# A selective-scan convolution block: another order of the small and full TensorE tiles, four PSUM banks in rotation, and three pieces of work moved between engines

## The chip, the cores and the metric

The kernel runs on one core of a Trainium2 chip. The metric is the device time of one execution in microseconds. A core has the engines TensorE (PE; its weight loads are shown apart as PEld), VectorE (DVE), ScalarE (ACT), GpSimd (POOL) and the DMA queues of SyncE (SP). Matmul results lie in PSUM, which this kernel uses as eight banks of 512 float32 for each of 128 partitions.

## The reference, cut to what matters

The input is `x` of shape (4, 128, 96, 96), float32. It is normalized by groups and flattened to sequences of 9216 positions in four directions (rows forward and back, columns forward and back). Each sequence goes through the block below; the four results are put back in place, multiplied by `fuse_w` and added to `x`.

```python
B, DIM, H, W = (4, 128, 96, 96)
HID, MH, G, K = (256, 32, 4, 5)
t = _grouped1x1(x, in_proj_w, in_proj_b, G)
u, gate = (t[:, :HID], t[:, HID:])
u = silu(u)
u = depthwise_conv(u, dw_w)                     # 5 taps along the sequence
s = _conv1x1(u, ssm_in_w)
a = DMIN + (DMAX - DMIN) * sigmoid(_conv1x1(u, ssm_delta_w, ssm_delta_b))
a = clip(a, 0.0001, 0.9999)
bb = tanh(_conv1x1(u, ssm_b_w, ssm_b_b))
cc = tanh(_conv1x1(u, ssm_c_w, ssm_c_b))
# hst[l] = a[l] * hst[l-1] + bb[l] * s[l]       (written with cumsum of logs)
u = u + _conv1x1(cc * hst + ssm_d[None, :, None] * s, ssm_out_w)
u = _grouped1x1(u * sigmoid(gate), mix_w, mix_b, G)
return _conv1x1(u, out_proj_w, out_proj_b)
```

## The kernel before

The weights of the last three products (mix, out_proj, fuse) are multiplied once at the start into `w_fin`. The work is then cut into units of N = 384 positions by 128 or 256 channels. Two units of opposite direction, s = 0 and s = 1, make a pair; there are 192 pairs, 48 per batch element, and `p` counts the four pairs of a step, on whose end a scan over the step's positions depends. In each batch element the first 24 pairs ("V") go along columns, the last 24 ("H") along rows. The loop is software pipelined: pair t does the convolution, projections and the scan's inputs of pair t, the output side (gate, `ssm_out`, gating) of pair t - LAG with LAG = 6, and the final product of the pair before that.

The order of each engine is that of the program text (it is scheduled by hand). A matmul of `mm` uses 32 columns of the array; its height is that of the operand: 32 rows in `rows` and `ssm_out`, 128 or 64 in `conv`, 128 in `proj` and `accumulate`. A float32 matmul shows as two records in the trace. All the `mm` calls are on one line, L129.

```python
SSM, TAPS, GATE = 0, 0, (2, 3)          # psum banks
REST = ((4, 5), (6, 7))

def rows(i, bi, banks):                 # in_proj: front half of unit i, gate of unit bi
    ...
    for c in range(4):
        for j in range(2):
            if i is not None:
                ...
                mm(bank(banks[0][j]), c, wn[r, 32 * m : 32 * m + 32], x_in[s][r, q, :], True, True)
            if bi is not None:
                ...
                mm(bank(banks[1][j]), c, gwn[r, 32 * c : 32 * c + 32],
                   x_in[bu["s"]][r, gq, off : off + N], True, True)
    # then on ScalarE: two Tanh of the gate into gv (L359), two Silu into sil (L370)
    ...

def ssm_out(bi):                        # 16 matmuls of 32x32 into banks 0 to 3
    ...

def add_u(bi):                          # L399, both units in one instruction
    pz = psum[:, SSM : SSM + 4, :N]
    nc.vector.tensor_add(pz, pz, us[bi].rearrange("p s j n -> p (s j) n"))

def gating(bi, s):                      # L404
    v = units[bi + s]["v"]
    pz = psum[:, SSM + 2 * s : SSM + 2 * s + 2, :N]
    nc.vector.scalar_tensor_tensor(v, v, 1.0, pz, ALU.add, ALU.mult)

def conv(i, banks):                     # half of the channels: band matmuls, then two copies to u (L426)
    ...

def taps(i, ks):                        # the other half: tap 0 on ScalarE (L440), taps 1 to 4 on DVE (L442),
    part = psum[:, TAPS : TAPS + 2, :N] # with the partial sum in banks 0 and 1
    ...

def proj(i, banks):                     # B, a, s and C of the pair
    ...                                 # 16 matmuls, then
    nc.scalar.activation(ta[:, p, :], pa, AF.Tanh, bias=b_proj[:, 0:1])              # L468, ta has a stride of R = 4
    nc.scalar.copy(tb[0:64, p, :], pb[0:64, :])                                      # L469, s
    nc.scalar.activation(tb[64:P, p, :], pb[64:P, :], AF.Tanh, bias=b_proj[64:P, 1:2])  # L470
    ...
    nc.gpsimd.tensor_scalar(a, a, half, DMIN + half, ALU.mult, ALU.add)              # L473
    nc.gpsimd.tensor_scalar(a, a, 0.9999, 0.0001, ALU.min, ALU.max)                  # L474
    nc.gpsimd.tensor_mul(ta[0:64, p, :], tb[0:64, p, :], ta[0:64, p, :])             # L475
    nc.gpsimd.tensor_scalar_mul(tb[0:64, p, :], tb[0:64, p, :], d_sb[0:64, :])       # L476, d*s

def scan(step, part):                   # DVE, L494: half a step, in the first two pairs of the next step
    ...
def outputs(step, p):                   # GpSimd, L500 to L502: C*h, + d*s, a copy
    ...

def accumulate(bu, bk):                 # the product with w_fin, added to acc in SBUF
    ...
    y, add = py[:, :N], nc.vector.tensor_add
    if s == 0:                          # unit s = 0: copy out (L517 or L519), add on GpSimd
        ys = wk.tile([P, N], F32, tag="ys", name=f"ys_{bu['id']}")
        ...
        y, add = ys, nc.gpsimd.tensor_add
    else:                               # unit s = 1 ("r"): add on DVE out of PSUM
        y, p, st = y[:, ::-1], R - 1 - p, NS - 1 - st
    ...                                 # L528 ("V") or L532 ("H")

def pair(t):
    i, k, bi = 2 * t, t % R, 2 * (t - LAG)
    ...
    front_banks, conv_banks = REST[t % 2], REST[1 - t % 2]
    rows(front, back, (front_banks, GATE))
    taps(i, range(1, K))
    conv(i, conv_banks)
    recurrence(t)                       # scan (k < 2) and outputs
    ...
    rows(front + 1, bi + 1, (front_banks, GATE))
    if waiting and (bi == 2 or (bi - 2) % (NU // B)):
        accumulate(waiting.pop(0), conv_banks[0])
        if len(waiting) > 1 and units[bi]["st"] == 1:
            accumulate(waiting.pop(0), conv_banks[1])
    ssm_out(bi)
    add_u(bi)
    if later:                           # a piece of the next batch element's statistics
        small[0] = front_banks[1]
        next(later[0], None)
    for s in range(2):
        gating(bi, s)
    proj(i, (conv_banks[1], front_banks[0]))
    first_tap(i + 2)
    if waiting:
        accumulate(waiting.pop(0), front_banks[1])
    waiting.extend(units[bi : bi + 2])
```

(In `pair` the tests for the first and last pairs are cut.) When a batch element is done, its result is written from `acc` to memory and `acc` is loaded with the next one's `x`; the `if` before the first `accumulate` puts off the first unit of a new batch element, and the one below it catches up a few pairs later.

Of the kernel before, what the change touches and what calls it, by code (L numbers as in the profile page):

```python
# [34 lines left out]
F32 = mybir.dt.float32  # L35
I32 = mybir.dt.int32
AF = mybir.ActivationFunctionType
ALU = mybir.AluOpType

P = 128  # L40
B, DIM, HH, WW = 4, 128, 96, 96
# [3 lines left out]
DMIN, DMAX = 0.999, 0.9999  # L45
# [5 lines left out]
N = LN * WW // R  # L51
M = WW // R
LAG = 6
# [4 lines left out]
def conv_preact_kernel(  # L58
# [20 lines left out]
    nc = tc.nc  # L79
# [16 lines left out]
    units = []  # L96
# [19 lines left out]

    psum = ps.tile([P, 8, 512], F32, name="psum")
    SSM, TAPS, GATE = 0, 0, (2, 3)  # L120
    REST = ((4, 5), (6, 7))
    LAST = ((4, 5), (6, 7))

    def bank(i):
        return psum[:, i, :]

    def mm(o, col, lhsT, rhs, start, stop):
        r = slice(32 * col, 32 * col + 32)
        nc.tensor.matmul(o[r, : rhs.shape[-1]], lhsT, rhs, start=start, stop=stop,  # L129
                         skip_group_check=True)  # L130
# [263 lines left out]
                    mm(bank(SSM + 2 * s + j), c, w_so[r, 128 * j + 32 * c : 128 * j + 32 * c + 32],  # L394
                       z[r, p, :], True, True)

    def add_u(bi):
        pz = psum[:, SSM : SSM + 4, :N]
        nc.vector.tensor_add(pz, pz, us[bi].rearrange("p s j n -> p (s j) n"))  # L399

    def gating(bi, s):
        v = units[bi + s]["v"]
        pz = psum[:, SSM + 2 * s : SSM + 2 * s + 2, :N]
        nc.vector.scalar_tensor_tensor(v, v, 1.0, pz, ALU.add, ALU.mult)  # L404

    us = {}

    def conv(i, banks):

        un = units[i]  # L410
        sil, p = sils[un["step"]], un["p"]
        small = 1 if p < 2 else 0

        def part(s, k, g, r, start):
            mm(bank(banks[s]), g, band[r, s, p, k, g, :], sil[r, s, 0, g, k : k + N],
               start, not start)

        for s in range(2):
            for g in range(4):
                part(s, 1 - small, g, slice(0, P), True)  # L420
        for g in range(4):
            for s in range(2):
                low = 64 * ((small + s + 1) % 2)
                part(s, small, g, slice(low, low + 64), False)
        for s in range(2):
            nc.scalar.copy(us[i][:, s, 0, :], bank(banks[s])[:, :N])  # L426
# [27 lines left out]
    def proj(i, banks):  # L454

        step, p = units[i]["step"], units[i]["p"]
        if step not in scans:
            scans[step] = [
                wk.tile([P, N, R], F32, tag="t0", name=f"t0_{step}").rearrange("p n r -> p r n"),
                wk.tile([P, R, N], F32, tag="t1", bufs=3, name=f"t1_{step}"),  # L460
            ]
        ta, tb = scans[step]
        for j in (1, 0):
            for bk, cols in zip(banks, ((qb, qb, qa, qa), (qs, qs, qc, qc))):
                for c in range(4):
                    mm(bank(bk), c, w_proj[:, j, cols[c]], us[i][:, c % 2, j, :], j == 1, j == 0)
        pa, pb = (bank(bk)[:, :N] for bk in banks)
        nc.scalar.activation(ta[:, p, :], pa, AF.Tanh, bias=b_proj[:, 0:1])  # L468
        nc.scalar.copy(tb[0:64, p, :], pb[0:64, :])  # L469
        nc.scalar.activation(tb[64:P, p, :], pb[64:P, :], AF.Tanh, bias=b_proj[64:P, 1:2])  # L470
        a = ta[64:P, p, :]
        half = (DMAX - DMIN) / 2
        nc.gpsimd.tensor_scalar(a, a, half, DMIN + half, ALU.mult, ALU.add)  # L473
        nc.gpsimd.tensor_scalar(a, a, 0.9999, 0.0001, ALU.min, ALU.max)  # L474
        nc.gpsimd.tensor_mul(ta[0:64, p, :], tb[0:64, p, :], ta[0:64, p, :])  # L475
        nc.gpsimd.tensor_scalar_mul(tb[0:64, p, :], tb[0:64, p, :], d_sb[0:64, :])  # L476

    def first_tap(i):
        if i < NU:
            new_u(i)  # L480
            taps(i, range(1))
# [21 lines left out]

    reload = []

    def accumulate(bu, bk):
        b, s, p, st = bu["b"], bu["s"], bu["p"], bu["st"]
        py = bank(bk)
        for j in range(2):
            for c in range(4):  # L510
                mm(py, c, w_fin[:, bu["dir"], j, 32 * c : 32 * c + 32], bu["v"][:, j, :],
                   j == 0, j == 1)
        y, add = py[:, :N], nc.vector.tensor_add
        if s == 0:
            ys = wk.tile([P, N], F32, tag="ys", name=f"ys_{bu['id']}")
            if bu["order"] == "V":
                nc.scalar.copy(ys, y)  # L517
            else:
                nc.scalar.activation(ys, y, AF.Identity, bias=b_fin)  # L519
            y, add = ys, nc.gpsimd.tensor_add  # L520
        else:
            y, p, st = y[:, ::-1], R - 1 - p, NS - 1 - st
        if bu["order"] == "V":
            part = acc.rearrange("p (m q) r c -> p m q r c", q=R)[
                :, :, p, :, bass.ds(st * LN // R, LN // R)
            ]
            y = y.rearrange("p (c r m) -> p m r c", r=R, m=M)
            add(part, y, part)  # L528
            return
        part = acc[:, bass.ts(st, LN), p, :]  # L530
        y = y.rearrange("p (h m) -> p h m", m=M)
        add(part, y, part)  # L532
        if bu["st"] >= NS // 2 and bu["p"] == R - 1:

            halves = [bass.ts(2 * st + e, LN * WW // 2) for e in range(2)]
            for r in halves:
                nc.sync.dma_start(out[b, :, r], accf[:, r])
            reload.extend(halves)
            if s == 1:
                if b + 1 < B:  # L540
                    for r in reload:
                        nc.sync.dma_start(accf[:, r], xr[b + 1, :, r])
                reload.clear()
# [6 lines left out]
    def recurrence(t):  # L550
        i, k = 2 * t, t % R
        if k < 2 and 0 <= t // R - 1 < NU // UB:
            scan(t // R - 1, k)
        if 0 <= i - 10 < NU:
            outputs(units[i - 10]["step"], units[i - 10]["p"])

    def pair(t):
        i, k, bi = 2 * t, t % R, 2 * (t - LAG)
        front = i + UB if i + UB < NU else None
        back = bi if bi >= 0 else None  # L560
        front_banks, conv_banks = REST[t % 2], REST[1 - t % 2]
        rows(front, back, (front_banks, GATE))
        taps(i, range(1, K))
        conv(i, conv_banks)
        recurrence(t)
        un = units[i]
        if un["order"] == "V" and un["b"] + 1 < B and k > 1:
            for e in range(2):
                stats_chunk(un["b"] + 1, un["st"] * R + 2 * (k - 2) + e)
            if un["st"] == NS - 1 and k == R - 1:  # L570
                later[:] = [stats_finish(un["b"] + 1, nc.gpsimd)]
        if back is None:
            first_tap(i + 2)
        if front is not None or back is not None:
            rows(None if front is None else front + 1, None if back is None else bi + 1,
                 (front_banks, GATE))

        if waiting and (bi == 2 or (bi - 2) % (NU // B)):
            accumulate(waiting.pop(0), conv_banks[0])
            if len(waiting) > 1 and units[bi]["st"] == 1:  # L580
                accumulate(waiting.pop(0), conv_banks[1])
        if back is not None:
            ssm_out(bi)
            add_u(bi)
            if later:
                small[0] = front_banks[1]
                next(later[0], None)
            for s in range(2):
                gating(bi, s)
        proj(i, (conv_banks[1], front_banks[0]))  # L590
        if back is not None:
            first_tap(i + 2)
        if waiting:
            accumulate(waiting.pop(0), front_banks[1])
        if back is not None:
            waiting.extend(units[bi : bi + 2])

    def last_pair(t):

        bi = 2 * (t - LAG)  # L600
        recurrence(t)
        for s in range(2):
            rows(None, bi + s, (None, LAST[s]))
        ssm_out(bi)
        add_u(bi)
        for s in range(2):
            if len(waiting) > 1 - s:
                accumulate(waiting.pop(0), LAST[0][s])
            gating(bi, s)
        waiting.extend(units[bi : bi + 2])  # L610

# [6 lines left out]
    with tc.manual_schedule(  # L618
        engines={nc.tensor.engine, nc.vector.engine, nc.scalar.engine, nc.gpsimd.engine}
    ):  # L620
        for t in range(NU // 2):
            pair(t)
        for t in range(NU // 2, NU // 2 + LAG):
            last_pair(t)
        for s in range(2):
            accumulate(waiting.pop(0), LAST[0][s])


_NAMES = [
# [75 lines left out]
```

## Time and profile before

| | |
|---|---|
| time, median of 3 runs | 2121.9 us (2120.81 to 2121.96) |
| span of the profiled execution | 2121.0 us |
| granted TensorE clock | 0.994 |
| PE busy | 2074.4 us, 37072 matmul records |
| DVE busy | 1814.4 us |
| POOL busy | 1732.4 us |
| ACT busy | 1557.4 us |
| DMA | 133.89 MB, mean 63 GB/s |

The profile is of one execution. Its page gives the busy time of each engine, the span in 40 slices, the DMA queues, the chain of work that ended last (followed back from the last instruction, at each step to what released it), and the costliest groups of instructions: line, engine, operation, tiles written and read, shape, count, then busy time in us, the mean of one in ns, and the idle time of the engine just before them with what ended it. Finer views are the timeline (instructions of one engine in order of time: start, length, engine, line, operation, tiles, count, and idle time before), the waits (who waited for whom, in us, times, longest), and the groups. Ends of matmuls are modelled, and a PE that is called busy may still be filling or draining. Starts are the safer numbers.

### The profile page before, as it was taken

What the parts mean: (1) busy time and instruction counts of PE and PEld (TensorE: products, weight loads), DVE (VectorE), ACT (ScalarE), POOL (GpSimd) and SP (SyncE); (2) the same over time, 40 slices, a digit from 0 to 9 for tenths busy, and PEclk for the clock granted to TensorE, in tenths of its full rate; (3) what the DMA queues carried; (4) which work ended last, traced back from release to release, by engine and by line L of the source; (5) the groups of instructions that cost most, each with busy time, mean ns of one, the idle gap of its engine ahead of it and who ended that gap; (6) DMA issues with size and microseconds to landing.
All of it is one profiled execution on the core that took longest, in us unless ns stands there. A gap on an engine that the chain in (4) does not pass through costs nothing.

```text
span 2121.0 us, 83902 instructions
## 1 busy us (share of the span) xinstructions
PE 2074.4 (98%) x37072; PEld 666.1 (31%) x37072; DVE 1814.4 (86%) x1786; ACT 1557.4 (73%) x2899; POOL 1732.4 (82%) x1717
## 2 busy tenths in 40 slices
PE   5999999999999999999999999999999999999998
PEld 3233333333333333333332333333333333333323
DVE  4699998888888998888898899888888788888886
ACT  3777777777777777777777777777777677777763
POOL 4688888888887888888878888888888788888885
PEclk7999999999999999999999999999999999999999
DMA  5121211111542221111343221111134211111111
GB/s 159 50 66 51 58 51 43 36 44 46 149 128 59 58 64 38 39 41 44 96 117 108 59 67 42 43 37 44 36 103 125 71 36 44 38 43 36 36 50 71
DMA packets 83403, 133.89 MB, mean 63 GB/s; under 512 B 11616, under 2 KB 70624, under 8 KB 83040
## 3 DMA queue, kind: packets, MB, share of 16 engines
q1 hardware_dynamic: 81024, 127.64, 22.4%
q8 instruction: 291, 4.77, 1.0%
q10 hardware_dynamic: 2016, 0.90, 0.2%
q14 instruction: 72, 0.59, 0.1%
HBM read 109.62 MB, written 18.87 MB: 61 GB/s over the span
## 4 chain that ended last, share of the span: by engine, by line
PE 92%; DVE 3%; ACT 2%; POOL 1%; DMA 1%; issue 0%; ACTq 0%; SPq 0%; POOLq 0%; DVEq 0%
PE psum L129 91%; DVE t L494 1%; DVE psum L399 1%; DVE gv L404 1%; ACT t L468 0%; ACT sil L370 0%; DMA acc<-in_xr 0%; POOL t L475 0%; DMA b_mix<-in_mix_b 0%; ACT psum L440 0%; DVE psum L442 0%; POOL t L476 0%; POOL t L500 0%; POOL t L473 0%; POOL t L474 0%
## 5 line engine op out<-in xcount | busy, mean ns | idle before, releaser
L442 DVE SCALAR_TENSOR_TENSOR psum<-sil,w_tap,psum 128x768 f32<-128x768 f32 x576 | 589.1, 1023 | 103.3 <-ACT psum L440 89.3
L129 PE MATMUL psum<-gv,w_fin 128*32 128x384 f32 x6144 | 568.7, 489 | 1.3 <-DVE mean L177 1.0
L129 PE MATMUL psum<-u,w_proj 128*32 128x384 f32 x6144 | 536.5, 489 | 4.9 <-ACT sil L370 2.7
L359 ACT ACTIVATE gv<-psum,bnorm 128x384 f32<-128x384 f32 x768 | 403.2, 577 | 91.8 <-PE psum L129 79.3
L468 ACT ACTIVATE t<-psum,b_proj 128x384 f32<-128x384 f32 x192 | 193.9, 1010 | 369.6 <-PE psum L129 356.6
L129 PE MATMUL psum<-sil,band 128*32 128x384 f32 (+1 forms) x6144 | 445.4, 495 | 0.2
L399 DVE TENSOR_TENSOR psum<-psum,u 128x1536 f32<-128x1536 f32 x192 | 339.2, 1767 | 122.3 <-PE psum L129 62.8
L129 PE MATMUL psum<-x_in,wn 32*32 32x384 f32 (+1 forms) x12288 | 432.0, 498 | 7.2 <-DVE gv L404 4.2
L370 ACT ACTIVATE sil<-psum,bnorm 128x385 f32<-128x385 f32 x768 | 404.9, 587 | 13.0 <-DMA xs<-in_xr 10.8
L500 POOL TENSOR_TENSOR t<-t,t 64x384 f32<-64x384 f32 x192 | 242.6, 1264 | 155.6 <-DVE t L494 146.3
L404 DVE SCALAR_TENSOR_TENSOR gv<-gv,psum 128x768 f32<-128x768 f32 x384 | 349.4, 950 | 6.4
L501 POOL TENSOR_TENSOR t<-t,t 64x384 f32<-64x384 f32 x192 | 290.6, 1514 | 15.0
L129 PEld LDWEIGHTS psum<-gv,w_fin 128*32 128x32 f32 x6144 | 180.3, 109 | 343.1 <-issue 220.5
L129 PEld LDWEIGHTS psum<-u,w_proj 128*32 128x32 f32 x6144 | 179.8, 109 | 343.5 <-issue 309.4
L473 POOL TENSOR_SCALAR t<-t 64x384 f32<-64x384 f32 x192 | 187.1, 975 | 100.2 <-ACT t L468 88.6
L476 POOL TENSOR_SCALAR t<-t,d_sb 64x384 f32<-64x384 f32 x192 | 240.5, 1253 | 19.8
L475 POOL TENSOR_TENSOR t<-t,t 64x384 f32<-64x384 f32 x192 | 237.0, 1234 | 15.4
L129 PEld LDWEIGHTS psum<-sil,band 128*32 128x32 f32 (+1 forms) x6144 | 114.5, 107 | 318.1 <-issue 276.3
L129 PEld LDWEIGHTS psum<-x_in,wn 32*32 32x32 f32 x12288 | 124.5, 103 | 286.0 <-ACT sil L370 117.6
L129 PE MATMUL psum<-t,w_so 32*32 32x384 f32 x6144 | 198.0, 493 | 4.2 <-POOL t L500 3.9
L442 DVE SCALAR_TENSOR_TENSOR u<-sil,w_tap,psum 128x768 f32<-128x768 f32 x192 | 194.9, 1015 | 6.8
L474 POOL TENSOR_SCALAR t<-t 64x384 f32<-64x384 f32 x192 | 184.2, 960 | 15.9
(73 smaller groups left out, 1455.3 us busy)
## 6 DMA issues: line engine op xcount, KB each, us to landing
x_in<-in_xs SPq DMA_DIRECT2D x96, 385.0 KB, 4.3
x_in<-in_xs SPq DMA_DIRECT2D x384, 96.2 KB, 2.5
acc<-in_xr SPq DMA_DIRECT2D x48, 384.0 KB, 4.2
out<-acc SPq DMA_DIRECT2D x48, 384.0 KB, 3.2
xs<-in_xr SPq DMA_DIRECT2D x72, 192.0 KB, 3.1
w_fuse<-in_fuse_wT ACTq DMA_DIRECT2D x1, 256.0 KB, 7.3
w_proj<-in_proj_wT ACTq DMA_DIRECT2D x1, 128.0 KB, 4.8
w_so<-in_ssm_out_wT ACTq DMA_DIRECT2D x1, 128.0 KB, 2.6
```

The costliest lines, as they stand in the source:

```text
L129: nc.tensor.matmul(o[r, : rhs.shape[-1]], lhsT, rhs, start=start, stop=stop, skip_group_check=True)
L359: nc.scalar.activation(gv[:, j, :], bank(banks[1][j])[:, :N], AF.Tanh, bias=gbn[:, 2 + j : 3 + j], scale=0.5,)
L370: nc.scalar.activation(sil[:, j, g, :], bank(banks[0][j])[:, : N + 1], AF.Silu, bias=bn[:, 1:2] if j else bn[:, 4 + g : 5 + g],)
L399: nc.vector.tensor_add(pz, pz, us[bi].rearrange("p s j n -> p (s j) n"))
L404: nc.vector.scalar_tensor_tensor(v, v, 1.0, pz, ALU.add, ALU.mult)
L442: nc.vector.scalar_tensor_tensor(us[i][:, :, 1, :] if k == K - 1 else part, src, w_tap[:, k : k + 1], part, ALU.mult, ALU.add,)
L468: nc.scalar.activation(ta[:, p, :], pa, AF.Tanh, bias=b_proj[:, 0:1])
L473: nc.gpsimd.tensor_scalar(a, a, half, DMIN + half, ALU.mult, ALU.add)
L475: nc.gpsimd.tensor_mul(ta[0:64, p, :], tb[0:64, p, :], ta[0:64, p, :])
L476: nc.gpsimd.tensor_scalar_mul(tb[0:64, p, :], tb[0:64, p, :], d_sb[0:64, :])
L500: nc.gpsimd.tensor_mul(ta[0:64, p, :], tb[64:P, p, :], ta[64:P, p, :])
L501: nc.gpsimd.tensor_add(tb[0:64, p, :], ta[0:64, p, :], tb[0:64, p, :])
```

## The change

The change orders the work of a pair anew and moves three pieces of it.

- The first `accumulate` of a pair goes ahead of the second `rows`, into bank 2 (`GATE[0]`), and `ssm_out` comes directly behind that second `rows`: two bursts of 32x32 tiles without full tiles in between.
- Banks 4 to 7 go round by one a pair instead of being swapped by twos. The gate of the second `rows` goes to the banks of `conv`, and `proj` uses these two as well.
- `add_u` is gone; `gating` adds u for its own unit, so that there are two additions of half the size, each in front of its product.
- The product d*s moves from GpSimd to ScalarE and into the next pair (`scale_s`), behind the second `rows`.
- In the loop the unit s = 1 ("r") is now also copied out by ScalarE and added on GpSimd, not on DVE. In the last pairs (`direct`) the addition is on DVE.
- The first Tanh of `proj` goes to a new contiguous tile `tm`; the three instructions behind it read `tm` and write `ta`.
- `proj` begins with j = 0 instead of j = 1, and `first_tap` of the next pair comes ahead of `proj`.
- At a batch change the late unit is caught up with at the end of the same pair (`late`), and the statistics' pieces run only in pairs without a scan, behind `proj`.

```diff
-    SSM, TAPS, GATE = 0, 0, (2, 3)
-    REST = ((4, 5), (6, 7))
+    SSM, TAPS, GATE, REST = 0, 0, (2, 3), 4
...
-    def add_u(bi):
-        pz = psum[:, SSM : SSM + 4, :N]
-        nc.vector.tensor_add(pz, pz, us[bi].rearrange("p s j n -> p (s j) n"))
-
     def gating(bi, s):
         v = units[bi + s]["v"]
         pz = psum[:, SSM + 2 * s : SSM + 2 * s + 2, :N]
+        nc.vector.tensor_add(pz, pz, us[bi][:, s])
         nc.vector.scalar_tensor_tensor(v, v, 1.0, pz, ALU.add, ALU.mult)
...
-        for j in (1, 0):
+        for j in range(2):
...
-        nc.scalar.activation(ta[:, p, :], pa, AF.Tanh, bias=b_proj[:, 0:1])
+        tm = wk.tile([P, N], F32, tag="tm", name=f"tm_{units[i]['id']}")
+        nc.scalar.activation(tm, pa, AF.Tanh, bias=b_proj[:, 0:1])
...
-        nc.gpsimd.tensor_scalar(a, a, half, DMIN + half, ALU.mult, ALU.add)
+        nc.gpsimd.tensor_scalar(a, tm[64:P, :], half, DMIN + half, ALU.mult, ALU.add)
         nc.gpsimd.tensor_scalar(a, a, 0.9999, 0.0001, ALU.min, ALU.max)
-        nc.gpsimd.tensor_mul(ta[0:64, p, :], tb[0:64, p, :], ta[0:64, p, :])
-        nc.gpsimd.tensor_scalar_mul(tb[0:64, p, :], tb[0:64, p, :], d_sb[0:64, :])
+        nc.gpsimd.tensor_mul(ta[0:64, p, :], tb[0:64, p, :], tm[0:64, :])
+
+    def scale_s(i):
+        s = scans[units[i]["step"]][1][0:64, units[i]["p"], :]
+        nc.scalar.activation(s, s, AF.Copy, scale=d_sb[0:64, 0:1])
...
-    def accumulate(bu, bk):
+    def accumulate(bu, bk, direct=False):
...
-        if s == 0:
+        if not direct or (s == 0 and bu["order"] == "H"):
             ys = wk.tile([P, N], F32, tag="ys", name=f"ys_{bu['id']}")
-            if bu["order"] == "V":
+            if s == 0 and bu["order"] == "H":
+                nc.scalar.activation(ys, y, AF.Identity, bias=b_fin)
+            else:
                 nc.scalar.copy(ys, y)
-            else:
-                nc.scalar.activation(ys, y, AF.Identity, bias=b_fin)
-            y, add = ys, nc.gpsimd.tensor_add
-        else:
+            y = ys
+            if not direct:
+                add = nc.gpsimd.tensor_add
+        if s == 1:
             y, p, st = y[:, ::-1], R - 1 - p, NS - 1 - st
...
-        front_banks, conv_banks = REST[t % 2], REST[1 - t % 2]
+        rest = [REST + (t + e) % 4 for e in range(4)]
+        conv_banks, front_banks = rest[:2], rest[2:]
+
+        late = bi > 2 and (bi - 2) % (NU // B) == 0
         rows(front, back, (front_banks, GATE))
         taps(i, range(1, K))
         conv(i, conv_banks)
+        if back is None:
+            first_tap(i + 2)
         recurrence(t)
...
-        if back is None:
-            first_tap(i + 2)
+        if waiting and not late:
+            accumulate(waiting.pop(0), GATE[0])
         if front is not None or back is not None:
             rows(None if front is None else front + 1, None if back is None else bi + 1,
-                 (front_banks, GATE))
-
-        if waiting and (bi == 2 or (bi - 2) % (NU // B)):
-            accumulate(waiting.pop(0), conv_banks[0])
-            if len(waiting) > 1 and units[bi]["st"] == 1:
-                accumulate(waiting.pop(0), conv_banks[1])
+                 (front_banks, conv_banks))
+        if t > 0:
+            scale_s(i - 2)
         if back is not None:
             ssm_out(bi)
-            add_u(bi)
-            if later:
-                small[0] = front_banks[1]
-                next(later[0], None)
             for s in range(2):
                 gating(bi, s)
-        proj(i, (conv_banks[1], front_banks[0]))
-        if back is not None:
             first_tap(i + 2)
+        proj(i, conv_banks)
+        if later and k > 1:
+            small[0] = front_banks[1]
+            next(later[0], None)
+        if late:
+            accumulate(waiting.pop(0), front_banks[1])
         if waiting:
-            accumulate(waiting.pop(0), front_banks[1])
+            accumulate(waiting.pop(0), front_banks[0])
...
-            add_u(bi)
...
-                accumulate(waiting.pop(0), LAST[0][s])
+                accumulate(waiting.pop(0), LAST[0][s], True)
```

More of the change, by code (lines that the diff above doesn't have):

```diff
@@ L462, in proj @@
         ta, tb = scans[step]
-        for j in (1, 0):
+        for j in range(2):
             for bk, cols in zip(banks, ((qb, qb, qa, qa), (qs, qs, qc, qc))):
                 for c in range(4):
-                    mm(bank(bk), c, w_proj[:, j, cols[c]], us[i][:, c % 2, j, :], j == 1, j == 0)
+                    mm(bank(bk), c, w_proj[:, j, cols[c]], us[i][:, c % 2, j, :], j == 0, j == 1)
         pa, pb = (bank(bk)[:, :N] for bk in banks)
-        nc.scalar.activation(ta[:, p, :], pa, AF.Tanh, bias=b_proj[:, 0:1])
+        tm = wk.tile([P, N], F32, tag="tm", name=f"tm_{units[i]['id']}")
+        nc.scalar.activation(tm, pa, AF.Tanh, bias=b_proj[:, 0:1])
         nc.scalar.copy(tb[0:64, p, :], pb[0:64, :])
@@ L600, in last_pair @@
         bi = 2 * (t - LAG)
+        if bi + 2 * LAG == NU:
+            scale_s(NU - 2)
         recurrence(t)
@@ L625, in conv_preact_kernel @@
         for s in range(2):
-            accumulate(waiting.pop(0), LAST[0][s])
+            accumulate(waiting.pop(0), LAST[0][s], True)
 _NAMES = [
```

## The prediction

> **What bounds the kernel now.** I read the page first: the busy table, the chain that ended last, the costliest groups.
>
> ```profile
> PE 2074.4 (98%) x37072; PEld 666.1 (31%) x37072; DVE 1814.4 (86%) x1786; ACT 1557.4 (73%) x2899; POOL 1732.4 (82%) x1717
> ...
> PE 92%; DVE 3%; ACT 2%; POOL 1%; DMA 1%; issue 0%; ACTq 0%; SPq 0%; POOLq 0%; DVEq 0%
> ...
> L399 DVE TENSOR_TENSOR psum<-psum,u 128x1536 f32<-128x1536 f32 x192 | 339.2, 1767 | 122.3 <-PE psum L129 62.8
> L404 DVE SCALAR_TENSOR_TENSOR gv<-gv,psum 128x768 f32<-128x768 f32 x384 | 349.4, 950 | 6.4
> ...
> L476 POOL TENSOR_SCALAR t<-t,d_sb 64x384 f32<-64x384 f32 x192 | 240.5, 1253 | 19.8
> ```
>
> TensorE is "busy" for 98% and holds 92% of the last chain, so only what shortens TensorE's time per pair counts. The loop runs 192 pairs. The other engines have room: DVE 86%, POOL 82%, ACT 73%. But a busy PE is not a PE that streams, so the second view is the timeline of TensorE over one pair in steady state. Columns: start, length, engine, line, operation, tiles, count.
>
> ```profile
> 439.95 0.95 PE L129 MATMUL psum<-t,w_so 32*32 32x384 f32 x32
> 440.83 2.79 PE L129 MATMUL psum<-u,w_proj 128*32 128x384 f32 x32
> 443.43 1.47 PE L129 MATMUL psum<-gv,w_fin 128*32 128x384 f32 x16
> 444.84 0.94 PE L129 MATMUL psum<-x_in,wn 32*32 32x385 f32 x32
> 445.71 2.31 PE L129 MATMUL psum<-sil,band 128*32 128x384 f32 x32
> 447.95 1.01 PE L129 MATMUL psum<-x_in,wn 32*32 32x385 f32 x32
> 448.89 1.50 PE L129 MATMUL psum<-gv,w_fin 128*32 128x384 f32 x16
> 450.31 0.95 PE L129 MATMUL psum<-t,w_so 32*32 32x384 f32 x32
> ```
>
> The pair lasts 450.31 - 439.95 = 10.36 us. How much of it streams? Inside a burst of full-height tiles, four weight loads follow each other every 0.32 us (409.58, 409.90, 410.22 in the timeline of the weight loads), so four column tiles side by side take 0.32 us. Then w_proj (32 records, 8 rounds) is 2.56 us, two w_fin bursts (4 rounds each) 2.56, the band 4 full rounds plus 2 of half-height tiles 1.92, and three bursts of 32x32 tiles (16 side by side, 2 rounds each) 1.92. Together 8.96 us. The other 1.40 us of a pair are the seven places where the tile size changes (small to full, full to half, half to small, small to full, full to small, small to full, full to small): 0.20 each on average. Single ones, from starts of bursts less the rounds: small to full 0.23 to 0.30, the others 0.14 to 0.17.
>
> The third view is DVE in a pair with a scan, and the burst of small tiles behind it.
>
> ```profile
> 418.55 1.81 DVE L494 TENSOR_TENSOR_SCAN t<-t,t 64x768 f32<-64x768 f32 x1
> 420.40 1.77 DVE L399 TENSOR_TENSOR psum<-psum,u 128x1536 f32<-128x1536 f32 x1
> 422.20 1.82 DVE L404 SCALAR_TENSOR_TENSOR gv<-gv,psum 128x768 f32<-128x768 f32 x2
> ```
>
> ```profile
> 418.71 0.94 PE L129 MATMUL psum<-t,w_so 32*32 32x384 f32 x32
> ...
> 423.60 1.41 PE L129 MATMUL psum<-x_in,wn 32*32 32x385 f32 x32
> ...
> 429.54 0.94 PE L129 MATMUL psum<-t,w_so 32*32 32x384 f32 x32
> ```
>
> Gating ends at 422.20 + 1.82 = 424.02, but rows, which writes its gate into banks 2 and 3, has begun at 423.60 and must wait inside the burst: 1.41 us instead of 0.94, and the pair takes 10.83. So there is a second loop close below TensorE's own: ssm_out, addition of u, gating, next rows. In the quiet pair the addition starts 1.18 us after ssm_out (441.13), gating ends 4.80 after it (442.93 + 1.82 = 444.75), and rows starts 4.89 after it (444.84): in time by 0.09. Comparing all pairs, rows is held back as soon as gating ends later than some 0.05 us before rows' start, and then one for one. A step of four pairs takes 10.36, 10.36, 10.82, 10.42: 10.49 on average, 0.13 of it from the scans.
>
> **What the Trainium skill says.** "TensorEngine Tiling (Array Packing)", Key Properties: changing the tiling mode, not just the tile, drains TensorE. The trace agrees: 0.14 to 0.30 us per change, and none between w_proj and w_fin. "PSUM — Partial Sum Buffer", Specifications (TRN2): GpSimd can't access PSUM, so a result that GpSimd is to add has to be copied out first; in the trace every accumulation of GpSimd reads ys. "ScalarE: Activation LUTs", What ACT_TABLE_LOAD costs: an ACTIVATE costs 0.833 ns per element plus 280 ns with one pointer operand, some 93 ns of which overlap with the next; for 384 elements 600 ns, the trace has 596 (L519) and 577 (L359). L468 with the same size takes 1010: it writes with a stride of R elements.
>
> **The change, part by part.** *Order on TensorE.* A pair was: rows, band, rows, w_fin, ssm_out, w_proj, w_fin. It becomes: rows, band, w_fin, rows, ssm_out, w_proj, w_fin. The second rows and ssm_out are both 32x32, so one change of size goes (small to full after rows, up to 0.30; half to full replaces half to small). From starts in the quiet pair: ssm_out follows rows at 0.64 (its two rounds); w_proj another 0.88; w_proj and w_fin to rows 4.01; rows 0.87; band 2.24; w_fin 1.42. Sum 10.06 us, against 10.36: TensorE's own loop gets 0.30 shorter.
>
> *DVE.* The addition over 1536 is split in two of 768. The addition at 384 takes 555 ns (L532 on DVE) and at 1536 1767, so 768 should take 555 + 384 x 1.052 = 959. Chain: 0.96 + 0.03, 0.91, 0.96 + 0.03, 0.95 = 3.84 us, against 3.62 now (4.80 - 1.18). Gating would end 1.18 + 3.84 = 5.02 after ssm_out, rows could start at 4.89: with the 0.05 from above rows waits some 0.18 us in every pair. In return DVE loses the accumulation W of r (0.56 a pair), and the first tap moves to ScalarE's stretch before w_proj's results, so the taps are ready when gating ends. Taps then run 4.2 us, a scan 1.84: they end 5.02 + 4.2 + 1.84 = 11.1 after ssm_out, where the next addition isn't due before 10.24 + 1.18 = 11.4. So the scans stop delaying gating: the 0.13 goes.
>
> *ScalarE.* Added: d*s (64x384, 0.5 to 0.6) and a second ys (0.49 to 0.60). Removed: L468 writes contiguous tm, 1.01 to about 0.58. Sum: 1557/192 = 8.1 now, 8.1 + 0.55 + 0.5 - 0.43 = 8.7 of 10.2. In order it just fits: w_proj's three results end 5.5 after ssm_out, ys 6.0, and the next rows' results are due about 6.2.
>
> *GpSimd.* d*s goes (1.25), an addition comes (1.02 at "H", 1.22 at "V"), L473 reads contiguous data: 9.0 now, some 8.7 then. Fits.
>
> *Batch change.* Now ssm_out starts 618.26, 628.93, 640.88, 654.12: 10.67, 11.95, 13.24, and 10.8 follows; about 4.7 us over the mean, three times. The doubled accumulations on DVE go, but the first addition of the new batch still waits for the reload (the DMAs land around 627), now on GpSimd. I give 1.7 us back per change. The statistics' pairs (289.18 to 301.91 is 12.73 us) also cost some 4.6 us, three times; moved off the scan pairs they should lose 1.
>
> *Sum.* Steady: 10.06 + 0.18 = 10.24 instead of 10.49. From the first ssm_out (98.4) to the last full pair (2068.9) lie 185 pairs: 185 x 0.25 = 46. Batch 3 x 1.7 = 5, statistics 3 x 1 = 3, tail 0 (direct additions keep DVE there). 54 less than 2121.9 is 2068; I take 2070 for small new waits.
>
> **The rivals.** (1) *ScalarE becomes the bound.* Its first tap now waits for gating of s = 0 ahead of w_proj's results, which come out a microsecond later; everything behind slides. For it: only 0.2 us of slack before rows' results. Against it: 8.7 of 10.2 busy, and L468 gets cheap. It would make pairs of 10.4 or so: 185 x 0.1 = 18 less, with the batches about 2098. (2) *GpSimd becomes the bound*, by later work (L468 later), the wait for the scan (146.3 us of idle time before L500 now) and the reload at a batch change, with only two ys buffers that ScalarE then waits for. Steady pairs have some 1.5 us of room, so it would show only at the batches: plus 10, 2080. (3) *The DVE wait is not there*, if the addition starts earlier (half of ssm_out is enough for s = 0) or overlaps: pairs of 10.06, 185 x 0.43 = 80 less, 2037 to 2045. (4) *PSUM takes the place*: w_fin in bank 2 must be read by ScalarE before ssm_out writes there; ys ends about as ssm_out arrives. A 0.1 us wait a pair would make 2088.
>
> **Range and chances.** 2070 lies just 0.4% below the limit of 2% (2079.5). Rival 3 is worth 30 us below, rivals 1, 2 and 4 10 to 28 above. Range 2043 to 2102; faster by over 2% 0.66, within 2% 0.29, slower 0.05, as nothing in the change adds work to TensorE.
>
> **What would show it.** Right: TensorE's timeline with rows and ssm_out 0.64 apart; pairs of 10.2 with and without scan; gating's last end at or after the start of rows; the addition at 0.96; L468 near 0.58; DVE idle less before the addition. Wrong: waits of TensorE for ScalarE's ys or t, ScalarE without gaps, GpSimd behind by a pair, or 128x768 additions well over 1 us.

## The result and the profile after

The changed kernel takes 2121.3 us (median of 4 runs, 2119.8 to 2122.7), the kernel before 2121.8 (4 runs on the same chip). The ratio is 0.9999, 95% interval 0.9981 to 1.0016: no difference. The prediction said 2070.

No engine has become a new limit. First the page of the kernel after: the busy table, the chain that ended last, and the two groups of gating (addition and product). Then, from the groups with shapes kept apart, the two pieces of work that ScalarE does in a new way (columns as on the page: busy us, mean ns of one, idle us before it).

```profile
PE 2076.1 (98%) x37072; PEld 722.7 (34%) x37072; DVE 1760.7 (83%) x1800; ACT 1674.3 (79%) x3276; POOL 1630.4 (77%) x1703
...
PE 94%; DVE 4%; DMA 1%; ACT 1%; issue 1%; ACTq 0%; DVEq 0%; SPq 0%; POOL 0%
...
L400 DVE TENSOR_TENSOR psum<-psum,u 128x768 f32<-128x768 f32 x384 | 369.6, 963 | 225.6 <-PE psum L129 224.4
L401 DVE SCALAR_TENSOR_TENSOR gv<-gv,psum 128x768 f32<-128x768 f32 x384 | 366.6, 955 | 43.3 <-ACT sil L370 0.9
```

```profile
L477 ACT ACTIVATE t<-t,d_sb 64x384 f32<-64x384 f32 x192 | 117.7, 613 | 1.3 <-POOL t L473 1.3
...
L466 ACT ACTIVATE tm<-psum,b_proj 128x384 f32<-128x384 f32 x192 | 108.2, 564 | 1.9 <-PE psum L129 1.9
```

DVE and GpSimd have become lighter, ScalarE heavier, each as intended. DVE now idles 225.6 us before the addition (122.3 before the change), nearly all of it for TensorE: the prediction had expected less. TensorE is "busy" as long as before, with the same number of matmuls. The time must lie inside its bursts, so here is its timeline over a quiet pair (start, length, engine, line, operation, tiles, count).

```profile
442.49 0.94 PE L129 MATMUL psum<-x_in,wn 32*32 32x385 f32 x32
443.16 1.30 PE L129 MATMUL psum<-t,w_so 32*32 32x384 f32 x32
444.39 2.79 PE L129 MATMUL psum<-u,w_proj 128*32 128x384 f32 x32
447.00 1.47 PE L129 MATMUL psum<-gv,w_fin 128*32 128x384 f32 x16
448.40 0.98 PE L129 MATMUL psum<-x_in,wn 32*32 32x385 f32 x32
```

`ssm_out` follows the second `rows` at 0.67, as predicted. But `ssm_out` itself is 1.30 us long where it was 0.94, and `w_proj` starts 1.23 after it, not 0.88. From `rows` to `w_proj` it is 1.90 us. The two bursts with full tiles between them cost 0.94 + 0.88 = 1.82 before. Putting them together saved nothing.

The starts of single matmul records show where this lies. The table is worked out from the trace, in us after the start of the burst, median of the burst in every full pair.

| record | `ssm_out` before | `rows`, `ssm_out` after | `ssm_out` twice (e2) |
|---|---|---|---|
| first burst: 1st to 16th | 0 to 0.119 | 0 to 0.118 | 0 to 0.118 |
| first burst: 17th to 32nd | 0.347 to 0.464 | 0.348 to 0.463 | 0.347 to 0.463 |
| second burst: 1st | | 0.671 | 0.669 |
| second burst: 2nd | | 0.864 | 0.862 |
| second burst: then one every | | 0.0167 | 0.0167 |

Within the first burst the records follow each other by 0.0067 us at first. The second burst's first record starts at 0.67, about when two rounds of 0.32 are over; its second comes 0.19 later, about where full tiles would start (0.875 before). From there they come at less than half the pace.

Split by the starts of `ssm_out`, the two spans compare as follows (rounded; the first `ssm_out` before is at 98.7, not at the 98.4 of the prediction).

| us | before | after | difference |
|---|---|---|---|
| up to the first `ssm_out` | 98.7 | 92.6 | -6.1 |
| 185 full pairs | 1970.3 | 1958.7 | -11.5 |
| the rest, the last six pairs | 52.1 | 66.8 | +14.7 |
| span | 2121.0 | 2118.1 | -2.9 |

Pairs take 10.48 us instead of 10.36, a pair with a delaying scan 10.65 ("H") or 10.85 ("V"). Against the median pair at the same place of a step, a batch change costs 0.5 us instead of 4.7, and the pairs with statistics 6.5 us in all instead of 12.6. The tail gave back more than the loop had gained.

### The profile page after: what moved, and what is told of

It reads as the page before. It is cut to its first block, busy times and chain, and to the rows that moved or that the text cites. A ratio compares the mean times of both kernels' runs of the same rounds, so it can differ in the third digit from the quotient of the medians.

```text
span 2118.1 us, 84825 instructions
## 1 busy us (share of the span) xinstructions
PE 2076.1 (98%) x37072; PEld 722.7 (34%) x37072; DVE 1760.7 (83%) x1800; ACT 1674.3 (79%) x3276; POOL 1630.4 (77%) x1703
## 4 chain that ended last, share of the span: by engine, by line
PE 94%; DVE 4%; DMA 1%; ACT 1%; issue 1%; ACTq 0%; DVEq 0%; SPq 0%; POOL 0%
PE psum L129 93%; DVE psum L400 1%; DVE gv L401 1%; DVE psum L439 0%; DVE t L495 0%; DMA acc<-in_xr 0%; DVE acc L535 0%; DMA b_mix<-in_mix_b 0%; DMA w_in<-in_in_wT 0%; ACT ys L518 0%; ACT t L468 0%; ACT sil L370 0%; DVE u L439 0%; ACT t L467 0%; ACTq L251 0%
## 5 line engine op out<-in xcount | busy, mean ns | idle before, releaser
L400 DVE TENSOR_TENSOR psum<-psum,u 128x768 f32<-128x768 f32 x384 | 369.6, 963 | 225.6 <-PE psum L129 224.4
L359 ACT ACTIVATE gv<-psum,bnorm 128x384 f32<-128x384 f32 x768 | 403.9, 578 | 110.8 <-PE psum L129 95.1
L129 PE MATMUL psum<-x_in,wn 32*32 32x384 f32 (+1 forms) x12288 | 412.5, 498 | 11.1 <-DVE acc L535 8.3
L370 ACT ACTIVATE sil<-psum,bnorm 128x385 f32<-128x385 f32 x768 | 405.7, 588 | 11.9 <-DMA xs<-in_xr 9.1
L401 DVE SCALAR_TENSOR_TENSOR gv<-gv,psum 128x768 f32<-128x768 f32 x384 | 366.6, 955 | 43.3 <-ACT sil L370 0.9
L471 POOL TENSOR_SCALAR t<-tm 64x384 f32<-64x384 f32 x192 | 176.4, 919 | 237.1 <-ACT tm L466 196.6
L501 POOL TENSOR_TENSOR t<-t,t 64x384 f32<-64x384 f32 x192 | 246.1, 1282 | 118.2 <-DVE t L495 106.8
L502 POOL TENSOR_TENSOR t<-t,t 64x384 f32<-64x384 f32 x192 | 287.5, 1497 | 15.1
L129 PE MATMUL psum<-t,w_so 32*32 32x384 f32 x6144 | 258.9, 495 | 1.7 <-DVE gv L401 1.7
L437 ACT ACTIVATE psum<-sil,w_tap 128x768 f32<-128x768 f32 x192 | 174.2, 907 | 107.1 <-DVE gv L401 70.6
L531 POOL TENSOR_TENSOR acc<-ys,acc 128x384 f32<-128x384 f32 x192 | 235.8, 1229 | 8.2 <-DMA x_in<-in_xs 0.6
L473 POOL TENSOR_TENSOR t<-t,tm 64x384 f32<-64x384 f32 x192 | 197.7, 1030 | 15.4
L423 ACT COPY u<-psum 128x384 f32<-128x384 f32 x384 | 165.4, 483 | 48.3 <-PE psum L129 48.0
```

The source lines that it names most:

```text
L359: nc.scalar.activation(gv[:, j, :], bank(banks[1][j])[:, :N], AF.Tanh, bias=gbn[:, 2 + j : 3 + j], scale=0.5,)
L370: nc.scalar.activation(sil[:, j, g, :], bank(banks[0][j])[:, : N + 1], AF.Silu, bias=bn[:, 1:2] if j else bn[:, 4 + g : 5 + g],)
L400: nc.vector.tensor_add(pz, pz, us[bi][:, s])
L437: nc.scalar.activation(part, src, AF.Copy, scale=w_tap[:, 0:1])
L471: nc.gpsimd.tensor_scalar(a, tm[64:P, :], half, DMIN + half, ALU.mult, ALU.add)
L473: nc.gpsimd.tensor_mul(ta[0:64, p, :], tb[0:64, p, :], tm[0:64, :])
```

## The experiments

**e1_tail: the tail alone.** In the last pairs `direct` puts the addition of y on DVE. Where the unit s = 0 belongs to "H", y is still copied out by ScalarE first. From the waits of the kernel after (waiter, awaited, us, times, longest), and from DVE's timeline in the last pairs (the bracket is the idle time before, with its cause):

```profile
DVE acc L535 <- ACT ys L518: 19.3, 6, 4.7
```

```profile
2071.88 0.56 DVE L535 TENSOR_TENSOR acc<-ys,acc 128x384 f32<-128x384 f32 x1 [2.95 <-ACT ys L518]
2072.36 0.95 DVE L400 TENSOR_TENSOR psum<-psum,u 128x768 f32<-128x768 f32 x1
```

DVE works in order, so gating of the next pair stands behind an addition that waits for a copy. The edit gives that addition back to GpSimd:

```diff
-        if not direct or (s == 0 and bu["order"] == "H"):
+        if not direct or s == 0:
...
-            if not direct:
-                add = nc.gpsimd.tensor_add
+            add = nc.gpsimd.tensor_add
```

> The changed kernel, but in the last six pairs the accumulation of s = 0 is added on GpSimd again and that of s = 1 on DVE straight from PSUM, as before the change. The changed kernel's end, from the last full pair's ssm_out (2051.3) to the end of the span (2118.1), takes 66.8 us, where it took 52.1 before the change. Theory T (direct additions behind ScalarE's ys put DVE's gating behind a chain of w_fin, ys and addition): the end takes 51 to 55 us again, so about 2107. Rival (the split additions or d*s make the end longer): 2119 to 2123 as it was.

Measured: 2107.8 us, ratio 0.9943 [0.9928, 0.9958]. The rest behind the last full pair is 52.7 us instead of 66.8, and between the starts of `ssm_out` the last pairs take 6.2 to 6.3 us where they took 7.5 to 9.6. The tail's loss was this one wait.

**e2_twice: the cost of a small burst behind a small burst, by itself.** The kernel before with `ssm_out` issued a second time, same operands, same banks, so the second burst has nothing to wait for.

```diff
             ssm_out(bi)
+            ssm_out(bi)
             add_u(bi)
```

> The kernel before, with ssm_out issued twice in succession in each full pair: the same matmuls into the same banks, no wait between the two, so this measures what a burst of 32x32 tiles costs directly behind another one. Theory A (the second of two small bursts is not fed until the first has left the array, so it costs as much as one behind a change of tile size): about 1.02 us a pair, as ssm_out costs in the changed kernel's 1.90 us for rows and ssm_out together less 0.88 for rows alone; 185 x 1.02 = 189, less up to 24 because the scans then no longer delay gating: 2287 to 2311, and ssm_out to w_proj 1.9 us. Theory B (the changed kernel's ssm_out waits for another engine, ScalarE's ys above all; bursts in succession stream without a gap): 0.64 us a pair, 2216 to 2240, and ssm_out to w_proj 1.52 us.

Timeline of TensorE, the two bursts as one line, and the next:

```profile
645.57 1.92 PE L129 MATMUL psum<-t,w_so 32*32 32x384 f32 x64
647.42 2.79 PE L129 MATMUL psum<-u,w_proj 128*32 128x384 f32 x32
```

From `ssm_out` to `w_proj` 1.85 us instead of 0.87: the second burst costs 0.98, not the 0.64 of its two rounds, and its records start like those of the kernel after (table above). One run took 2274.2 us. The sum agrees: 186 pairs x 0.98 = 182, less 24 because the longer pairs hide the scans, less 5 in the pairs with statistics for the same reason, is 153; measured 2274.2 - 2120.7 = 153.5. So the extra time needs no wait for another engine. Nor is it the banks: here both bursts write the same ones, in the kernel after they write different ones, and the starts are the same.

**e11_inter: the same 32 matmuls, interleaved.** As e2, but each matmul is issued twice in a row.

```diff
-    def ssm_out(bi):
+    def ssm_out(bi, times=1):
...
-                    mm(bank(SSM + 2 * s + j), c, w_so[r, 128 * j + 32 * c : 128 * j + 32 * c + 32],
-                       z[r, p, :], True, True)
+                    for _ in range(times):
+                        mm(bank(SSM + 2 * s + j), c,
+                           w_so[r, 128 * j + 32 * c : 128 * j + 32 * c + 32],
+                           z[r, p, :], True, True)
...
-            ssm_out(bi)
+            ssm_out(bi, 2)
```

> The kernel before, with each matmul of ssm_out issued twice in succession, so that a tile's second matmul follows its first at once instead of a whole burst later. The earlier run with two whole bursts cost 0.98 us a pair. If only the order of a whole burst behind a burst keeps the weights from being loaded ahead, this costs 0.64 us a pair and w_proj follows ssm_out's start by 1.52 us: about 2121 + 182 x 0.64 - 24 = 2213. If any second matmul on a tile that is still busy stops what is behind it, it costs 0.98 or more: 2274 or, if the tiles then run one after another, several hundred us more.

From `ssm_out` to `w_proj` 3.11 us, a pair 12.59, one run 2504.9 us. That is 2.23 a pair over the kernel before, more than twice the price of e2. That fits a second matmul for a busy tile holding back those behind it, although their tiles are free; the trace doesn't name the tile of a record, so this is inferred from the time alone.

**e5_souter: could it be a wait for ys?** Rival 4 said that `ssm_out` waits for ScalarE to read y out of bank 2. Here `ssm_out` does all of s = 0 (banks 0 and 1) first, so banks 2 and 3 come into play half a burst later.

```diff
-        for c in range(4):
-            for s in range(2):
+        for s in range(2):
+            for c in range(4):
```

> The changed kernel with ssm_out's matmuls ordered by unit first (all of s = 0, banks 0 and 1, then s = 1, banks 2 and 3) instead of by column. Bank 2, which ScalarE's ys must have read, is needed eight matmuls later. Theory B (ssm_out waits for ys in bank 2): the gap of 0.19 us between ssm_out's first and second matmul goes, pairs get up to 0.2 us shorter, 2080 to 2100. Theory A (it waits for the burst ahead): the gap stays, pairs 10.4 to 10.5, as the addition for s = 0 may start a little earlier; 2110 to 2122.

Measured: 2115.8 us, 0.9975 [0.9964, 0.9985]. The second record of `ssm_out` still starts 0.864 after `rows`, the gap is unmoved, and rival 4 falls. In the kernel after, too, the 0.864 is the same in "V" and "H", where ys ends between 0.62 and 0.78 after the start of `rows`. The small gain is another thing: the addition of s = 0 starts 1.16 after `ssm_out` instead of 1.26, `rows` after gating isn't held back any more (0.87 to the band, where after has 0.91 to 0.94), and quiet pairs take 10.42 to 10.45, those with a delaying scan 10.76 to 11.01.

**e6_both: e1 and e5 together.**

> The changed kernel with both gains so far: the end as before the change, and ssm_out ordered by unit. If the two are independent (13.5 and 5.6 us off the changed kernel's 2121.3), 2102; if the order by unit only shifts the wait, 2106 to 2109.

Measured: 2101.1 us, 0.9912 [0.9896, 0.9929]. The two gains add up.

**e9_outputs: the scans.** Back to the kernel after, a pair with a scan: DVE, then GpSimd in the same stretch.

```profile
451.48 1.01 DVE L439 SCALAR_TENSOR_TENSOR u<-sil,w_tap,psum 128x768 f32<-128x768 f32 x1
452.52 2.51 DVE L495 TENSOR_TENSOR_SCAN t<-t,t 64x768 f32<-64x768 f32 x1
455.07 0.97 DVE L400 TENSOR_TENSOR psum<-psum,u 128x768 f32<-128x768 f32 x1
```

```profile
452.17 1.26 POOL L501 TENSOR_TENSOR t<-t,t 64x384 f32<-64x384 f32 x1
453.51 2.54 POOL L502 TENSOR_TENSOR t<-t,t 64x384 f32<-64x384 f32 x1
```

The scan is 2.51 us long instead of the 1.81 seen before; L501 was running when it began and ends at 453.43. L502, begun inside the scan, needs 2.54, twice its usual time, and ends only after it. It looks as if one waited for the other. e9 is e6 with the outputs of a step's first pair issued on GpSimd behind an addition that waits for ys, so that they come after the scan.

```diff
+        if k or not t < NU // 2:
+            outputs_of(i)
...
         if waiting and not late:
             accumulate(waiting.pop(0), GATE[0])
+        if k == 0:
+            outputs_of(i)
```

> As the one before, but in each step's first pair GpSimd makes the outputs (L501 to L503 in the changed kernel) behind the addition of ys instead of ahead of it, so that it is idle when DVE's scan begins. In the changed kernel that scan takes 2.5 to 2.7 us where the second half's takes 1.81, with a GpSimd multiplication of two SBUF tensors running when it starts. Theory S (DVE's scan with two SBUF inputs and GpSimd's instruction exclude each other for the length of an instruction, and this is why scan pairs are still 0.2 to 0.5 us longer): the first scan takes about 1.85, scan pairs fall from 10.8 to 11.0 to about 10.45 or 10.5, and 45 of them make 12 to 20 us: 2084 to 2092. Rival (the scan is long because of its operands or a wait for its inputs): scan pairs stay, 2100 to 2106.

From the groups with shapes kept apart, e9 (busy us, mean ns of one, idle us before):

```profile
L502 POOL TENSOR_TENSOR t<-t,t 64x384 f32<-64x384 f32 x192 | 234.0, 1219 | 15.0
...
L495 DVE TENSOR_TENSOR_SCAN t<-t,t 64x768 f32<-64x768 f32 x40 | 75.3, 1881 | 3.4 <-POOL t L473 2.1
```

and the same two groups after:

```profile
L502 POOL TENSOR_TENSOR t<-t,t 64x384 f32<-64x384 f32 x192 | 287.5, 1497 | 15.1
...
L495 DVE TENSOR_TENSOR_SCAN t<-t,t 64x768 f32<-64x768 f32 x40 | 100.2, 2505 | 3.1 <-POOL t L473 1.9
```

The scan falls from 2505 to 1881 ns on average and the usual pairs take 10.42 to 10.45, with a scan or without. Measured: 2088.3 us, 0.9849 [0.9835, 0.9864]. "GPSIMD Engine Reference", 8. Key points, in the Trainium skill, says that GpSimd and VectorE share their SBUF interfaces and contend when a VectorE instruction has two SBUF inputs. The trace agrees, and the size is near that of exclusion, each waiting for the rest of the other's instruction: when the scan began L501 had 0.91 us left, and the scan is 0.70 longer; when L502 began the scan had 1.52 left, and L502 is 1.32 longer.

**e3_order: the old order with the moved work.** If the burst order is the loss, the old order of TensorE with the work left where the change put it should gain. e3 is e1 with the banks, the order of `accumulate` and `rows`, the undivided addition, the order of j in `proj` and the place of `first_tap` as before; d*s, `tm`, the copies of r and the batch change stay as after.

```diff
-        rest = [REST + (t + e) % 4 for e in range(4)]
-        conv_banks, front_banks = rest[:2], rest[2:]
+        front_banks, conv_banks = halves[t % 2], halves[1 - t % 2]
...
-        if waiting and not late:
-            accumulate(waiting.pop(0), GATE[0])
...
-                 (front_banks, conv_banks))
+                 (front_banks, GATE))
+        if waiting and not late:
+            accumulate(waiting.pop(0), conv_banks[0])
...
             ssm_out(bi)
+            add_u(bi)
...
+        proj(i, (conv_banks[1], front_banks[0]))
             first_tap(i + 2)
-        proj(i, conv_banks)
```

> The changed kernel with TensorE's order, the bank pairs and the undivided addition of u as before the change, and the end as before; it keeps the work that the change moved (d*s on ScalarE, both accumulations in the loop on GpSimd, the contiguous tm, the batch change in one pair, the statistics in pairs without a scan). Theory A (the new order of tiles gains nothing by itself and costs 0.12 us a pair with the longer chain on DVE; the moves are worth having): pairs of 10.36 with and without a scan, or up to 0.1 more in scan pairs, instead of 10.48 and 10.65 to 10.85; with the shorter batch changes 2070 to 2085. Rival (the new order was what freed DVE, without it the scans delay gating as before the change, 10.82): 2095 to 2110.

Measured: 2125.4 us, 1.0021 [1.0011, 1.0031]: the expectation missed. Quiet pairs take 10.48 again, but for another reason, and pairs with a scan 10.9 ("H") to 11.1 ("V"). TensorE and ScalarE in e3:

```profile
437.89 1.13 PE L129 MATMUL psum<-x_in,wn 32*32 32x385 f32 x32
438.95 1.50 PE L129 MATMUL psum<-gv,w_fin 128*32 128x384 f32 x16
```

```profile
435.66 0.48 ACT L523 COPY ys<-psum 128x384 f32<-128x384 f32 x1
436.03 1.06 ACT L359 ACTIVATE gv<-psum,bnorm 128x384 f32<-128x384 f32 x2
436.97 1.07 ACT L370 ACTIVATE sil<-psum,bnorm 128x385 f32<-128x385 f32 x2
```

In the old order ScalarE's second copy (L523) stands right ahead of the gate's Tanh. L359 and L370 slide, L370 ends at 438.04, and the second `rows` that began at 437.89 takes 1.13 us instead of 1.01: 1.06 to `w_fin` instead of 0.94.

**e7_dve: e3 with r added on DVE again.** This takes that copy off ScalarE and, with it, the addition of r from GpSimd to DVE; nothing else changes.

```diff
-    def accumulate(bu, bk, direct=False):
+    def accumulate(bu, bk, direct=True):
```

> The kernel with the order before the change, with one more part undone: in the loop the accumulation of s = 1 (W of r) is on DVE straight from PSUM again. Theory E (the second ys of 0.48 us on ScalarE, ahead of the next pair's gates, made the pairs 10.48 and not 10.36): pairs without a scan are 10.36, scan pairs 10.8, and with the shorter batch changes 2095 to 2105. Rival (d*s on ScalarE is what makes it late): pairs stay at 10.48, 2120 to 2130.

Measured: 2096.2 us, 0.9885 [0.987, 0.99]. Quiet pairs take 10.36 and TensorE is back at 0.94:

```profile
441.43 1.01 PE L129 MATMUL psum<-x_in,wn 32*32 32x385 f32 x32
442.37 1.50 PE L129 MATMUL psum<-gv,w_fin 128*32 128x384 f32 x16
```

The way of r over GpSimd cost 0.12 a pair in this order; that it was the copy is read from ScalarE's timeline in e3, as no run moved the copy alone. Pairs with a scan fall to 10.64. The three batch changes now have a pair of 11.9, 12.4 and 14.0, as DVE's addition waits for the reload.

**e8_tap: e7 with the first tap between ScalarE's second and third result of `proj`,** so that DVE's taps may begin earlier.

```diff
         nc.scalar.copy(tb[0:64, p, :], pb[0:64, :])
+        first_tap(between)
         nc.scalar.activation(tb[64:P, p, :], pb[64:P, :], AF.Tanh, bias=b_proj[64:P, 1:2])
```

> As the one before, with the next pair's first tap put between ScalarE's second and third result of w_proj, so that DVE's taps start some 0.4 us earlier and the scan ends earlier. Theory E: pairs without a scan stay at 10.36, those with a scan fall from 10.8 to about 10.5: 2085 to 2095. Rival (the third result comes too late for the next band's bank, or gating of s = 0 holds the tap back): pairs of 10.4 to 10.5 throughout, 2105 to 2120.

Measured: 2091.2 us, 0.9867 [0.9852, 0.9882]. The step meant for the scans missed: they remain at 10.64 to 10.73. The gain over e7 in the median isn't explained: the two profiled executions, 2094.1 for e7 and 2094.7 here, don't show it. Why the scan pairs stayed can be read from the trace, DVE and then GpSimd:

```profile
411.50 2.10 DVE L500 TENSOR_TENSOR_SCAN t<-t,t 64x768 f32<-64x768 f32 x1
```

```profile
411.48 0.50 POOL L508 COPY t<-t 64x384 f32<-64x384 f32 x1
```

The first scan starts 0.58 us ahead of `ssm_out` instead of 0.37, but it now runs beside a GpSimd copy and takes 2.06 instead of 1.84 (medians). It ends where it ended in e7.

**e10_best: e8 with e9's move, and at a batch change both late units on GpSimd.**

```diff
+        if k == 0:
+            outputs_of(i)
...
-            accumulate(waiting.pop(0), front_banks[1])
+            accumulate(waiting.pop(0), front_banks[1], not late)
```

> As the kernel with the first tap between ScalarE's results (TensorE's order of before the change, W of r on DVE in the loop), with two more parts: in each step's first pair GpSimd makes the outputs behind the addition of ys, and at the batch change both late units are added on GpSimd. Theory S (the first scan and GpSimd's two-input instruction exclude each other): scan pairs fall from 10.67 to 10.36 to 10.4, 45 x 0.3 = 13 us. The batch changes (pairs of 12.3 to 14.4, DVE waiting for the reload ahead of the gating) fall to about 12: some 2 to 4 us each. Together 2068 to 2078. Rival (the scan pairs are held by something else, the batch changes by the transfer itself): 2085 to 2092.

Measured: 2082.9 us, 0.9822 [0.9806, 0.9838], a little above what was expected and the fastest of all. Quiet pairs take 10.36. The first scan starts as in e8 but takes 1.81, and pairs with a scan fall to 10.36 to 10.43, so it was GpSimd's work beside the scan that kept them long in e8. The pair of the batch change takes 12.0 instead of 12.3 to 14.4. TensorE in a pair of 10.36, from `ssm_out` to `ssm_out`:

```profile
463.51 0.94 PE L129 MATMUL psum<-t,w_so 32*32 32x384 f32 x32
...
468.39 0.95 PE L129 MATMUL psum<-x_in,wn 32*32 32x385 f32 x32
...
473.87 0.94 PE L129 MATMUL psum<-t,w_so 32*32 32x384 f32 x32
```

So the version that wins keeps TensorE's old order, d*s on ScalarE, the contiguous `tm` and the new batch change, and leaves out what the change was named for.

## Why the prediction was wrong, step by step

- **"ssm_out follows rows at 0.64 (its two rounds); w_proj another 0.88": this step failed.** The first half held (0.67), the second is 1.23. A burst of small tiles behind another of the same size was taken for two streaming rounds without a change of size; e2 measured 0.98 instead of 0.64. The general step, that a change of tile size drains and its absence doesn't, was drawn from full tiles: `w_fin` still follows `w_proj` at next to no cost (2.61 us after its start, where `w_proj`'s rounds are 2.56). TensorE's own loop is thus about 10.06 + 0.38 = 10.44, not 10.06.
- **"Rows waits some 0.18 us in every pair": about 0.05.** The addition was sized right (959 predicted, 963 measured), but `ssm_out` ends so late that the addition starts 0.03 after `w_proj` (444.42 against 444.39) and no longer 0.30 after it. The chain from there is 3.97, not 3.84, as each dependent product begins 1.07 to 1.08 after its addition, not 0.99. 10.44 + 0.05 is the 10.48 measured.
- **"The scans stop delaying gating": wrong.** The first scan takes 2.50 us ("H") and 2.72 ("V") instead of 1.84, by GpSimd's L501; with 1.84 it would have been over before the addition. e9 confirmed it. Once in four pairs 0.17 to 0.37 us.
- **"Tail 0 (direct additions keep DVE there)": wrong,** +14.7, the wait that e1 took away.
- **"1.7 back per change" of the batch: 4.2. "Statistics lose 1": 2.0.** Both were better than predicted. For the batch this fits e7 and e10, where the addition that waits for the reload is on DVE (11.9 to 14.0) and on GpSimd (12.0); for the statistics no run shows why.
- **ScalarE, DVE and GpSimd: right.** d*s 0.61, just above its 0.5 to 0.6, L466 0.56 for 0.58, ScalarE 8.7 a pair, GpSimd 8.5 for 8.7.
- **The rivals.** (1) and (2) didn't come: ScalarE and GpSimd have gaps; but a relative of (1) shows in e3, where, by its trace, the place of a short copy, not ScalarE's load, cost 0.12. (3) was half right, as the wait nearly vanished for a reason that cost more than it. (4) fell with e2 and e5.

The account, in us: 0.244 more a quiet pair than the predicted 10.24, x 185, is +45; the scans that still delay +8; batch changes and statistics -11, as they stand 11 above quiet pairs where the prediction's sum leaves 22; tail +15; start -6. Together +51: the predicted gain of 54 less the 3 by which the two spans differ. Why the start is 6 shorter isn't known; in the kernel after and e1, e5, e6 and e9, which leave it alone, it ends between 92.6 and 95.7.

What stays open is why the second small burst starts so late. "TensorE: Matmul & The Clock Gate", Part 3, The mechanism, in the Trainium skill, says that weight loads are pulled ahead of running matmuls if the row groups don't conflict or if the load goes to the background weight buffer. The tiles of `rows` use all four row groups, and the trace fits: of `ssm_out`'s 32 loads one starts at 0.35 and one at 0.67 after `rows` began, the other 30 from 0.86 on. That loads wait there for the tiles of the first burst fits e2 and e11, but it was only argued; no run changed the loads alone. Of the 15 us that e10 still has above 185 x 10.36, 9 lie in the pairs with statistics and 4 at the batch changes.

## What to carry to other kernels

A burst of small tiles behind a burst of the same small tiles isn't free because no tile size changes: measure one such pair by doubling a burst before reordering for it. Here the place of an instruction on its engine mattered more than its length: a copy of 0.48 us ahead of a gate, or an addition that waits ahead of gating, undid what was gained elsewhere. When a change bundles several moves, try each alone; here the minor ones, with waits at the scan, at the batch change and in the last pairs taken out, gave a kernel 1.8% faster, and the reordering that the change was named for gained nothing.

## What the runs showed of the hardware that was not expected

- Sixteen float32 matmuls of 32x32 tiles, N = 384, directly behind sixteen others cost 0.98 us against 0.64 by their rounds, and issue one record every 0.0167 us instead of 0.0067. Issued in twos on the same tile, the added sixteen cost 2.23 us.
- A DVE scan with two SBUF inputs and a GpSimd instruction that reads SBUF delay each other by most of what is left of the one that runs: the scan 1.81 to 2.51 us beside a multiplication and to 2.06 beside a copy, GpSimd's addition 1.22 to 2.54.
- A ScalarE Tanh of 384 elements takes 564 ns into a contiguous tile, where it took 1010 with a stride of four elements.
